# A recurrence on one core: the hidden product of half B from bf16 parts in every step, its input part placed by DMA, its gate product in fp32

## The chip, the core and the metric

The kernel runs on one core of one Trainium2 chip. Its time is the device time in microseconds, and the kernel before takes 1639.37 us, the median of three runs (1638.94 to 1640.77). The engines are TensorE (PE, with its weight loads as PEld), VectorE (DVE), ScalarE (ACT), GpSimd (POOL) and SyncE (SP), which only issues DMAs here.

## The reference

```
def step(h, x_t):                        # 512 steps, batch 8, 512 units
    fused = sigmoid(concat([x_t, h]) @ w_W + w_b)
    r, z = split(fused, 2)
    m = x_t @ wx_W + wx_b + r * (h @ wh_W + wh_b)
    return z * h + (1 - z) * tanh(m)
out = x + (h after every step)
```

Everything is fp32. Each step needs the state of the step before, so the 512 steps come one after the other; in each, the state (8 x 512) is multiplied with three 512 x 512 matrices (hh with wh_W, z and r with the lower half of w_W). The products of x need no state.

## The kernel before, in words

**Layout.** The 512 units are four chunks of 128 (k = 0 to 3 as inputs, j = 0 to 3 as outputs). Half A of the outputs is chunks 0 and 1 of the next state, half B chunks 2 and 3. The state is the stationary operand: 32 columns, which hold 4 steps x 8 batches, with zeros but for one step's eight. Output quarter j goes to rows 32j to 32j + 31 of a PSUM bank, so four quarters of the array work side by side, and a VectorE transpose of 128x64 in blocks of 32 turns the result back into the layout of the state. Four steps are a group g; a bank holds the x part of a group for all its four steps.

**Banks.** Per group and parity: A (192 columns: hh, z, r of half A), B (128 columns: r and hh of half B) and C (64 columns in the bank `cs`: z of half B). In odd groups C is fp32 like A and B. In even groups from step 24 on (`in_parts`, L500), C is made from bf16 parts (`parts`, L442): GpSimd splits the state into three bf16 parts, eight columns each (24 in all), TensorE multiplies these with the three parts of the weights (`wb`, `w2`, `w3`; one weight load, then three matmuls, two of them by `kept` without a load), and VectorE sums the parts after the transpose with a `tensor_reduce` (L692). Each step of such a group has its own cell in `cs`, filled beforehand with its x part times a mask (`spread_c`, L503).

**One step of TensorE** (L626 to 647): the products in the order `A0 B0 A1 A2 A3 B1 B2 B3 C0 C1 C2 C3` (bank, chunk of the state), then a share of the x products for later groups (`x_step`, L585). The share is by u, the step's number within eight: 384 columns for u = 0 to 3, 288 for u = 4 to 7 (`SHARE`). u = 0 to 3 are the even group of the eight steps, u = 4 to 7 the odd one.

**The recurrence** (L667 to 758): of each half, `turn_r`, `turn_h`, `turn_z` transpose on VectorE, and the two gates get their sigmoid on ScalarE. `memory` is a scan on VectorE over two slots for each unit: slot 0 starts from hh, slot 1 multiplies with r and adds the x part (`md0` holds 0 and r, `md1` holds hh and x), then a tanh on ScalarE. `update` is a scan that makes the new state in `hT`. `update(0, 0)` makes chunk 0, which A0 and B0 of the next step need; `update(0, 1)` chunk 1; `update(1, 0)` and `update(1, 1)` chunks 2 and 3. All of VectorE's, ScalarE's and SP's instructions run in program order.

**Between.** `spread` copies a group's x part into the banks (ScalarE), `turn_x` transposes the x part of m into `md1` (VectorE). Sums of x products go through `even` and `odd` in SBUF; the last addition for rows 64 to 127 of `even` is made by VectorE at u = 5, those for rows 0 to 63 by ScalarE at u = 2. The last two groups read PSUM directly (`source`). `Flow` (L92) plans the semaphores: for PSUM an instruction waits for the last access of every other engine to the same bank and rows; DMAs go round 24 lanes. All instructions of the loop are recorded under L255, so the tiles' names tell them apart: `tr`, `tz` are turned gates, `tzB` and `tzs` the turned and summed parts of C, `hd0` the sigmoid of z, `m` the scan's result.

Of the kernel before, what the change touches and what calls it, by code (L numbers as in the profile page):

```python
# [8 lines left out]
F32 = mybir.dt.float32  # L9
# [14 lines left out]
DVE_FILL = 14  # L24
IDLE = 3
ORDER = "A0 B0 A1 A2 A3 B1 B2 B3 C0 C1 C2 C3"

FIRST = "A0 A1 A2 A3 x x x x B0 B1 B2 B3 C0 C1 C2 C3"

BANKS = {"A": 192, "B": 128, "C": 64}  # L30
# [19 lines left out]
XP = {"A": slice(0, 192), "X": slice(192, 320), "C": slice(320, 384), "B": slice(384, 512)}  # L50
# [214 lines left out]
def tile_cond_rnn_residual(  # L265
# [105 lines left out]
    def wh(bank, k, j):  # L371
        return wa[:, k, j] if bank == "A" else wb[:, k, j, {"C": slice(0, 64), "B": slice(64, 192)}[bank]]
# [11 lines left out]
    split = [const.tile([P, NQ, 3, B], F32, name=f"split{i}") for i in range(2)]  # L384
    w2 = const.tile([P, NQ, NQ, HU], F32, name="w2")
    w3 = const.tile([P, NQ, NQ, HU], F32, name="w3")
    mask = const.tile([P, GS, 32], F32, name="mask")

    md0 = [[pair(n, f"md0{n}{i}", 32, 2) for i in range(2)] for n in "AB"]
    md1 = [[pair(n, f"md1{n}{i}", 32, 2) for i in range(2)] for n in "AB"]  # L390
# [12 lines left out]
    for n, t_ in enumerate(hd0[0] + hd0[1] + md0[0] + md0[1] + hs):  # L403
        (nc.vector if n < DVE_FILL else nc.gpsimd).memset(t_, 0.0)
    steps = const.tile([P, GS, 32], F32, name="steps")
    nc.vector.memset(steps, 0.0)
    for n in range(GS):
        nc.vector.memset(steps[:, n, B * n : B * n + B], 1.0)
    nc.vector.transpose(mask.rearrange("p s n -> p (s n)"), steps.rearrange("p s n -> p (s n)"))
# [12 lines left out]
    def state(hf, i, slot=2):  # L422
# [8 lines left out]
         "B": wide[q]["B"][:, : BANKS["B"]],  # L431
         "C": cs[:, GS * HU : GS * HU + HU]}
# [9 lines left out]
    def parts(out_, i, k, j):  # L442
        lhsT = high(split[i % 2])[:, k].rearrange("p u b -> p (u b)")[:, 1::2]
        for n, t_ in enumerate((wb[:, k, j, :HU], w2[:, k, j], w3[:, k, j])):
            (nc.tensor.kept if n else mm)(out_, lhsT, high(t_)[:, 1::2])
# [15 lines left out]
    bias = const.tile([P, 512], F32, name="bias")  # L461
    for hf in range(2):
# [40 lines left out]
    def spread_c(g, steps_):  # L503

        for s in steps_:
            nc.scalar.activation(
                cell(GS * g + s), source(g)[:, XP["C"]], AF.Copy, scale=mask[:, s, :1]
            )

    def turn_x(g, hf):  # L510

        c0 = XP["X"].start + HU * hf
        nc.vector.transpose(
            md1[hf][g % 2][:, :, :, 1].rearrange("p n c -> p c n"), source(g)[:, c0 : c0 + HU]
# [89 lines left out]
    for k in range(NQ):  # L604
        for g in range(3):
            take(first[g], 1)
        if k == 0:
            mm(wide[1]["B"], ones.rearrange("p j m -> p (j m)"), rows4, start=True)
            nc.vector.tensor_copy(bias, wide[1]["B"])
            for t_ in (even, odd):  # L610
# [3 lines left out]
    spread_c(0, range(GS))  # L614
    for hf in range(2):
        turn_x(0, hf)
    keep(1)
    keep(2)
# [4 lines left out]
    for i in range(T):  # L623
# [8 lines left out]
        for n in (ORDER if i else FIRST).split():  # L632
# [4 lines left out]
            lhsT = hs[i % NH][:, k, :32, 2]  # L637
            for j in range(NQ):
                if bank == "C" and in_parts(i):
                    parts(cell(i)[32 * j : 32 * j + 24], i, k, j)  # L640
                else:
                    to = cell(i) if bank == "C" else ps[bank]
                    mm(to[32 * j : 32 * j + 32, :], lhsT, wh(bank, k, j))
# [7 lines left out]
        def scan(c_, out_, d0, d1):  # L651
# [10 lines left out]
            "h": (pa[:, :HU], ps["B"][:, HU:]),  # L662
            "z": (pa[:, HU : 2 * HU], cell(i)),
# [281 lines left out]
```

## Time and profile before

| | |
|---|---|
| median of three runs | 1639.37 us |
| the profiled execution, whole | 1637.59 us |
| its span, first to last instruction | 1635.5 us |
| granted TensorE clock | 1.00 |
| TensorE busy | 1625.4 us |
| VectorE, ScalarE, GpSimd busy | 1235.8, 1254.0, 531.8 us |
| DMA: out, by 128 issues | 64 KB each, 1.6 us to landing |
| DMA: x, by 112 issues | 64 KB each, 2.4 us to landing |

A timeline row gives the start in us, the time from the first start to the last end of the instructions merged into it, the engine, the line, the operation, the tiles (out<-in), the shape and the count; a bracket at its end tells how long the engine stood idle before it and for whom. A row of groups gives, after the count, the busy time of all in us and the mean of one in ns, then the idle time before them.

### The profile page before, as it was taken

Reading aid. Unit: us, or ns where it says so; the run is one execution under the profiler, and the core shown is the slowest. Engines: PE = TensorE matmul, PEld = TensorE weight load, DVE = VectorE, ACT = ScalarE, POOL = GpSimd, SP = SyncE. Lnnn points to the kernel's source line nnn. Section 1 sums busy time; section 2 is a strip of 40 time slices with the busy share of each in tenths; the row PEclk is TensorE's granted clock in tenths of the full one; section 3 lists DMA queues with packets and bytes.
Section 4 is the critical chain, followed back from the end, with each engine's and each line's share of the span. In section 5 each row is a group of like instructions: output and inputs, shape, how many; then the busy total and the mean of one; then the engine's idle time right before and its main releaser. Section 6 shows DMA issues by size and latency. Waiting matters only on the chain.

```text
span 1635.5 us, 127307 instructions
## 1 busy us (share of the span) xinstructions
PE 1625.4 (99%) x58202; PEld 1397.4 (85%) x50394; DVE 1235.8 (76%) x9433; ACT 1254.0 (77%) x6188; POOL 531.8 (33%) x2272
## 2 busy tenths in 40 slices
PE   8999999999999999999999999999999999999998
PEld 5988898988888888888888888888888888988887
DVE  7777777777777777777777777777777777777776
ACT  4777777778777777777777777777777777777775
POOL 1323323333233333332333333323333333333332
PEclk9999999999999999999999999999999999999999
DMA  4000000000000000000000000000000000000000
GB/s 185 12 14 18 15 15 14 18 15 14 15 18 15 15 14 18 15 15 15 17 15 15 15 18 14 15 15 18 14 15 15 17 15 15 15 18 10 10 10 11
DMA packets 37297, 31.25 MB, mean 19 GB/s; under 512 B 4084, under 2 KB 35060, under 8 KB 36600
## 3 DMA queue, kind: packets, MB, share of 16 engines
q1 hardware_dynamic: 36576, 22.89, 4.5%
q8 instruction: 425, 6.96, 1.7%
q14 instruction: 144, 1.18, 0.2%
q10 hardware_dynamic: 152, 0.22, 0.0%
HBM read 14.70 MB, written 8.39 MB: 14 GB/s over the span
## 4 chain that ended last, share of the span: by engine, by line
PE 98%; DVE 1%; DMA 0%; ACT 0%; issue 0%; DVEq 0%; ACTq 0%; SPq 0%
PE A L255 41%; PE B L255 27%; PE xp L255 17%; PE cs L255 9%; PE cs L219 4%; PE eps L255 1%; DMA head<-in_xh_dram 0%; DVE tr L255 0%; DVE m L255 0%; DVE tw L255 0%; DVE hT L255 0%; DVE md1A L255 0%; DVE tz L255 0%; DVE md1B L255 0%; DVE even L255 0%
## 5 line engine op out<-in xcount | busy, mean ns | idle before, releaser
L255 PE MATMUL A<-wa,hT 128*32 128x192 f32 x16384 | 872.3, 327 | 3.2 <-DVE hT L255 3.1
L255 PEld LDWEIGHTS A<-wa,hT 128*32 128x32 f32 x16384 | 549.4, 122 | 189.8 <-DVE hT L255 132.1
L255 PE MATMUL B<-wb,hT 128*32 128x128 f32 x16384 | 652.0, 273 | 0.0
L255 PEld LDWEIGHTS B<-wb,hT 128*32 128x32 f32 x16384 | 542.5, 122 | 19.9 <-DMA wb<-in_wb_dram 0.3
L255 POOL TENSOR_TENSOR ot<-xin,hT 128x16 f32<-128x16 f32 x991 | 224.1, 250 | 598.8 <-DVE hT L255 596.8
L255 ACT ACTIVATE hT<-m 128x8 f32<-128x8 f32 x2048 | 349.2, 208 | 65.0 <-DVE m L255 64.1
L255 DVE STREAM_TRANSPOSE tr<-A 128x64 f32<-128x64 f32 x512 | 127.9, 250 | 291.9 <-PE A L255 285.8
L255 PE MATMUL xp<-tw,sx 128*32 128x384 f32 (+2 forms) x1464 | 264.0, 433 | 0.0
L255 POOL TENSOR_TENSOR split<-hT 128x32 f32<-128x32 f32 x488 | 126.0, 258 | 410.0 <-DVE m L255 397.9
L255 ACT ACTIVATE hT<-hT 128x16 f32<-128x16 f32 x1022 | 210.3, 225 | 50.1 <-DVE hT L255 47.8
L255 ACT ACTIVATE md0A<-tr 128x16 f32<-128x16 f32 x512 | 112.2, 219 | 165.4 <-DVE tr L255 158.8
L255 DVE TENSOR_TENSOR_SCAN hT<-hd0B,hT 128x24 f32<-128x24 f32 x1024 | 179.5, 204 | 75.7 <-ACT hT L255 52.4
L255 PE MATMUL xp<-wx,xin 128*32 128x384 f32 (+4 forms) x1348 | 218.3, 413 | 0.0
L255 DVE TENSOR_TENSOR_SCAN hT<-hd0A,hT 128x24 f32<-128x24 f32 x1024 | 198.3, 194 | 0.0
L255 PE MATMUL cs<-wb,hT 128*32 128x64 f32 x8576 | 173.0, 219 | 0.0
L255 PEld LDWEIGHTS cs<-wb,hT 128*32 128x32 f32 x8576 | 161.4, 122 | 0.0
L255 DVE TENSOR_TENSOR_SCAN m<-md0A,md1A 128x16 f32<-128x16 f32 x1024 | 142.3, 181 | 6.9
L255 DVE TENSOR_TENSOR_SCAN m<-md0B,md1B 128x16 f32<-128x16 f32 x1024 | 145.0, 163 | 0.6 <-issue 0.4
L255 ACT ACTIVATE hd0A<-tz 128x16 f32<-128x16 f32 x512 | 116.0, 227 | 20.9
L219 PE MATMUL cs<-w,split 128*24 128x64 bf16 x7808 | 129.9, 192 | 0.0
L255 PE MATMUL cs<-wb,split 128*24 128x64 bf16 x3904 | 122.2, 192 | 0.0
L255 POOL TENSOR_TENSOR split<-split 128x16 f32<-128x16 f32 x488 | 105.2, 216 | 38.2
(101 smaller groups left out, 2216.0 us busy)
## 6 DMA issues: line engine op xcount, KB each, us to landing
out_dram<-ot SPq DMA_DIRECT2D x128, 64.0 KB, 1.6
xin<-in_x_dram SPq DMA_DIRECT2D x112, 64.0 KB, 2.4
wx<-in_wx_dram SPq DMA_DIRECT2D x4, 768.0 KB, 7.5
wa<-in_wa_dram SPq DMA_DIRECT2D x4, 384.0 KB, 10.1
wb<-in_wb_dram SPq DMA_DIRECT2D x1, 1152.0 KB, 13.4
xin<-in_x_dram SPq DMA_DIRECT2D x3, 256.0 KB, 3.1
wb<-in_wb_dram SPq DMA_DIRECT2D x1, 384.0 KB, 13.8
head<-in_xh_dram ACTq DMA_DIRECT2D x1, 208.0 KB, 5.6
```

The source lines that it names most:

```text
L219: return t.add_instruction(mybir.InstMatmult(name=self.nc.get_next_instruction_name(), ins=[t.lower_ap(rhs), t.lower_ap(lhsT)], outs=[t.lo ...
L255: inst = getattr(self, item.op, getattr(engine, item.op, None))(*item.args, **item.kw)
```

## The change

- Bank B now holds z and r of half B, in fp32. The third product is H: hh of half B, into cells of `cs` (eight now, one for each step of eight). It is fp32 until step 23 and from parts in all steps from 24 on.
- The split state has four columns for each batch, (batch, part), the fourth zero: 32 columns instead of 24. GpSimd makes it in every step (before step 24 it copies the state into the second column).
- After the transpose a unit has four neighbouring slots. `memory` of half B is a scan over these four with factors 0, 1, 1 and r: it sums the three parts, multiplies with r and adds what stands in the fourth, which is the x part. The `tensor_reduce` goes, and so does the transpose of x of half B.
- The x part must stand in every fourth row of the cell. `move_x` sends 16 DMAs a group (4 steps x 4 quarters, 8 rows x 64 elements each) from `even` or `odd` to a tile `xz`, whose other rows hold the bias of hh in the first row of four and zeros. `fill(i + 2)` copies one 128x64 piece of `xz` to the cell on ScalarE, in every step, behind the last update; it takes the place of `spread_c` and of the copies of C.
- In each step `turn_z(1)` now stands before `update(0, 0)` and `turn_h(1)` behind it, the order of updates is the same in all steps. The third bias addition (`keep(2)`) moves from the start into step 1.

```diff
-ORDER = "A0 B0 A1 A2 A3 B1 B2 B3 C0 C1 C2 C3"
+ORDER = "A0 B0 A1 A2 A3 B1 B2 B3 H0 H1 H2 H3"
-BANKS = {"A": 192, "B": 128, "C": 64}
+BANKS = {"A": 192, "B": 128}
...
+    def products_h(i, k):
+        four = split[i % 2]
+        for j in range(NQ):
+            to = cell(i)[32 * j : 32 * j + 32]
+            if not in_parts(i):
+                mm(to, four[:, k].rearrange("p b u -> p (b u)"), wh("H", k, j))
+                continue
+            lhsT = high(four)[:, k].rearrange("p b u -> p (b u)")[:, 1::2]
+            for n, t_ in enumerate((wh("H", k, j), w2[:, k, j], w3[:, k, j])):
+                (nc.tensor.kept if n else mm)(to, lhsT, high(t_)[:, 1::2])
...
     def cell(i):
-        return cs[:, HU * (i % GS) : HU * (i % GS) + HU] if i // GS % 2 == 0 else banks[1]["C"]
+        return cs[:, HU * (i % NH) : HU * (i % NH) + HU]
     def in_parts(i):
-        return 3 * NH <= i < T and i // GS % 2 == 0
+        return 3 * NH <= i < T
+    def move_x(g):
+        at = (even, odd)[g % 2]
+        if source(g) is not at:
+            nc.scalar.copy(at[:, XP["M"]], source(g)[:, XP["M"]])
+        for s in range(GS):
+            for j in range(NQ):
+                r = 32 * j
+                (nc.sync if g or s else nc.scalar).dma_start(
+                    out=xz[g % 2][r + 3 : r + 32 : 4, s],
+                    in_=at[r + B * s : r + B * s + B, XP["M"]],
+                )
+    def fill(i):
+        if i < T:
+            nc.scalar.copy(cell(i), xz[i // GS % 2][:, i % GS])
...
         def memory(hf, q):
             c_ = slice(q, q + 1)
-            scan(c_, ms[hf], md0[hf][g % 2][:, rows], md1[hf][g % 2][:, rows])
-            act(state(hf, i, 1)[:, :, c_], ms[hf][:, :, c_, 1], AF.Tanh)
+            d1 = memB.rearrange("p c (n s) -> p n c s", s=4) if hf else md1[g % 2][:, rows]
+            scan(c_, ms[hf], md0[hf][g % 2][:, rows], d1)
+            act(state(hf, i, 1)[:, :, c_], ms[hf][:, :, c_, SL[hf] - 1], AF.Tanh)
...
         turn_r(1)
+        turn_z(1)
+        update(0, 0)
         turn_h(1)
-        update(0, 0)
...
+        nc.after(update(0, 1), r_done[1])
...
+        memory(1, 0)
+        memory(1, 1)
         update(1, 0)
         update(1, 1)
-        if 0 < o < LAST and u == 1:
-            spread(2 * o + 1, "C")
-        if nxt and u in (6, 7):
-            spread_c(2 * o + 2, (2 * u - 12, 2 * u - 11))
+        for n in (1, 2) if i == 0 else () if i == T - 6 else (i + 1, i + 2) if i == T - 5 else (i + 2,):
+            fill(n)
...
         if o == LAST:
             if u == 2:
+                move_x(2 * o + 1)
...
         elif u == 5:
             if sums:
                 nc.vector.tensor_tensor(even[HI, XC], reg(BE), both[HI], ALU.add)
+            if sums or o + 1 == LAST:
+                move_x(2 * o + 2)
...
         elif u == 7 and nxt:
             if o:
                 nc.scalar.copy(odd[LO, XC], reg(GA))
-            turn_x(2 * o + 2, 1)
+            if sums:
+                move_x(2 * o + 3)
```

More of the change, by code (lines that the diff above doesn't have):

```diff
@@ L402, in tile_cond_rnn_residual @@
     nc.scalar.activation(const.tile([P, 1], F32, name="table"), zeros[:, :1], AF.Sigmoid)
-    for n, t_ in enumerate(hd0[0] + hd0[1] + md0[0] + md0[1] + hs):
+    for n, t_ in enumerate(hd0[0] + hd0[1] + md0[0] + md0[1] + split + hs):
         (nc.vector if n < DVE_FILL else nc.gpsimd).memset(t_, 0.0)
[L405 to L409, printed above, removed]
+    for t_ in md0[1]:
+        nc.gpsimd.memset(t_[:, :, :, 1:3], 1.0)
+    fourth = const.tile([P, 32], F32, name="fourth")
+    nc.vector.memset(fourth, 0.0)
+    nc.vector.memset(fourth[:, ::4], 1.0)
+    nc.vector.transpose(mask, fourth)
     for t_ in hd0[0] + hd0[1]:
@@ L670, in turned @@
             return t_[:, :, rows], inst
+        memB = work.tile([P, 2, 32], F32, tag="memB", name=f"memB_{i}")
         r_done = [None, None]
```

156 lines of the change are left out of this document (71 added, 85 removed).

## The prediction

> **What bounds the kernel now.** I read the page first: the span, the busy shares and the chain that ended last.
>
> ```profile
> span 1635.5 us, 127307 instructions
> PE 1625.4 (99%) x58202; PEld 1397.4 (85%) x50394; DVE 1235.8 (76%) x9433; ACT 1254.0 (77%) x6188; POOL 531.8 (33%) x2272
> PE 98%; DVE 1%; DMA 0%; ACT 0%; issue 0%; DVEq 0%; ACTq 0%; SPq 0%
> ```
>
> TensorE is never idle and is 98% of the chain, so on this page the kernel is TensorE's stream, and any matmul time saved should come off the end. The next question is how far the recurrence, which runs beside that stream on VectorE and ScalarE, is from being the limit itself. So I read the timeline of TensorE over an fp32 step (u = 4 of the eight) and over a step that takes C from bf16 parts (u = 1):
>
> ```profile
> 714.91 0.62 PE L255 MATMUL cs<-wb,hT 128*32 128x64 f32 x31
> 715.36 0.41 PE L255 MATMUL xp<-tw,xin 128*32 128x288 f32 x2
> 715.85 0.55 PE L255 MATMUL A<-wa,hT 128*32 128x192 f32 x8
> 716.17 0.44 PE L255 MATMUL B<-wb,hT 128*32 128x128 f32 x8
> 716.39 1.20 PE L255 MATMUL A<-wa,hT 128*32 128x192 f32 x24
> 718.02 0.62 PE L255 MATMUL cs<-wb,hT 128*32 128x64 f32 x31
> ...
> 730.64 0.20 PE L255 MATMUL cs<-wb,split 128*24 128x64 bf16 x2
> 731.00 0.49 PE L255 MATMUL xp<-wx,xin 128*32 128x384 f32 x2
> 731.65 0.54 PE L255 MATMUL A<-wa,hT 128*32 128x192 f32 x8
> ```
>
> Starts matter here, since matmuls overlap. C in fp32 holds TensorE from 714.91 to 715.36, 0.45 us; from parts it holds it from 730.64 to 731.00, 0.36 us. The x work behind it takes 0.49 us (288 columns) in the one and 0.65 us (384 columns) in the other. A0 to the end of B is 718.02 - 715.85 = 2.17 us in both. So an fp32 step is 2.17 + 0.45 + 0.49 = 3.11 us, a parts step 2.17 + 0.36 + 0.65 = 3.18 us. The same from VectorE, by the first transpose of u = 0, of u = 4 and of the next u = 0:
>
> ```profile
> 727.07 0.25 DVE L255 STREAM_TRANSPOSE tr<-A 128x64 f32<-128x64 f32 x1 [0.80 <-PE A L255]
> ...
> 739.79 0.25 DVE L255 STREAM_TRANSPOSE tr<-A 128x64 f32<-128x64 f32 x1
> ...
> 752.22 0.25 DVE L255 STREAM_TRANSPOSE tr<-A 128x64 f32<-128x64 f32 x1 [0.81 <-PE A L255]
> ```
>
> The four parts steps take 12.72 us, 3.180 each, and the four fp32 steps 12.43 us, 3.108 each.
>
> Now the loop beside it: the end of A, VectorE's transposes and scans, the first new state, A0 of the next step, the end of A again. The last steps of the kernel have no x work left to fill TensorE, so there the loop alone sets the pace:
>
> ```profile
> 1622.06 0.55 PE L255 MATMUL A<-wa,hT 128*32 128x192 f32 x8 [0.24 <-DVE hT L255]
> 1625.14 0.55 PE L255 MATMUL A<-wa,hT 128*32 128x192 f32 x8 [0.24 <-DVE hT L255]
> ```
>
> These are fp32 steps, TensorE waits 0.24 us in each, and and A0 comes 3.08 us after A0. That is the row of the whole argument: taking matmuls away cannot bring an fp32 step below 3.08 us, and it stands at 3.108 already. Only 0.03 us of each is TensorE's to give.
>
> **Part by part. The product of half B.** From step 24 on, 244 steps had C from parts and 244 in fp32; now all 488 take it from parts. By the rows above, 0.45 - 0.36 = 0.09 us less of TensorE in each of the 244 that change (u = 4 to 7), 22 us if nothing else held them. z of half B now rides in bank B, which stays 128 columns wide: nothing there. The stationary part grows from 24 to 32 columns:
>
> ```profile
> L255 PEld LDWEIGHTS cs<-wb,split 128*24 128x24 bf16 x3904 | 107.4, 93 | 9.9
> ```
>
> A load stands before three matmuls on the same quarter of the array and runs under its neighbours. At worst the first of a step shows its longer length, 93 x 32/24 - 93 = 31 ns, in the 244 steps that TensorE still bounds: 0 to 7.6 us. I take 0, since the row's loads are covered; more columns cannot gain. [...]
>
> **The loop.** VectorE in the same fp32 step, and TensorE's weight load that follows:
>
> ```profile
> 715.25 0.23 DVE L255 STREAM_TRANSPOSE tr<-B 128x64 f32<-128x64 f32 x1
> 715.40 0.24 DVE L255 STREAM_TRANSPOSE md1B<-B 128x64 f32<-128x64 f32 x1
> 715.53 0.20 DVE L255 TENSOR_TENSOR_SCAN hT<-hd0A,hT 128x24 f32<-128x24 f32 x1
> 715.65 0.23 DVE L255 STREAM_TRANSPOSE tz<-cs 128x64 f32<-128x64 f32 x1
> 715.79 0.17 DVE L255 TENSOR_TENSOR_SCAN hT<-hd0A,hT 128x24 f32<-128x24 f32 x1
> ...
> 716.33 0.31 DVE L255 TENSOR_TENSOR_SCAN hT<-hd0B,hT 128x24 f32<-128x24 f32 x2 [0.20 <-ACT hT L255]
> ```
>
> ```profile
> 715.78 0.24 PEld L255 LDWEIGHTS A<-wa,hT 128*32 128x32 f32 x8 [0.25 <-DVE hT L255]
> ```
>
> The first update (715.53 to 715.73) lets A0's weights load, at 715.78, and A0 starts at 715.85. With C shortened TensorE would be ready for A0 at 715.85 - 0.09 = 715.76: it would stand waiting. In front of that update the change puts the transpose of z (from B, to a plain tile) where hh's stood (from B, into every second slot). After the plain ones the next instruction starts 0.15 us later (715.25 to 715.40, 715.65 to 715.79 is 0.14), after the slotted one 0.13 (715.40 to 715.53). So the update moves 0.02 us back, and the floor from 3.08 to 3.10 us. The four u = 4 to 7 steps then take 4 x 3.10 = 12.40 instead of 12.43 us: 61 x 0.03 = 1.8 us gained. Bounds: no delay at all, 3.08, 61 x 0.11 = 6.7 us gained; the 0.05 us more that a plain transpose could cost, 3.13, 61 x 0.09 = 5.5 us lost.
>
> **Behind the first update** lie the four-slot scans. Sixteen elements take 163 ns, 24 take 194:
>
> ```profile
> L255 DVE TENSOR_TENSOR_SCAN m<-md0B,md1B 128x16 f32<-128x16 f32 x1024 | 145.0, 163 | 0.6 <-issue 0.4 <-DVE tzB L255 0.2
> L255 DVE TENSOR_TENSOR_SCAN hT<-hd0A,hT 128x24 f32<-128x24 f32 x1024 | 198.3, 194 | 0.0
> ```
>
> Thirty-two are then 0.02 to 0.06 us longer than 16. They delay A2. In the fp32 step above both updates of half B are done at 716.64, and A2 starts one chunk of A after A1, at 716.39 + 0.32 = 716.71: the second of them has 0.07 us to spare and A2 needs only the first. Against A0, which now comes 0.02 us later in the loop, A2 keeps its place, so this is covered. If it were not, 0.04 us would come on 244 steps, 10 us. In the u = 0 to 3 steps the sum over the quarter (reduce) and a mixed order go away; A2 is sometimes late there, and 3.180 goes to 2.17 + 0.36 + 0.65 = 3.176 at best: 244 x 0.004 = 1.0 us gained.
>
> **ScalarE and the DMAs.** One 128x64 fill a step, against five pieces in eight steps before; TensorE's parts on POOL in every step, not every second, behind the update and done before H0 of the next step, with 67% of POOL free. The new wait is on ScalarE: fill(i+2) waits for four DMAs, and the state copies, the spreads and the next sigmoid are queued behind it; VectorE and then TensorE wait for that. It is tight at one place, u = 6 of each eight, whose x is finished by VectorE only in u = 5:
>
> ```profile
> 719.78 0.56 DVE L255 TENSOR_TENSOR even<-xp,both 64x384 f32<-64x384 f32 x1
> ```
>
> ```profile
> 714.25 0.33 SPq L255 DMA_DIRECT2D out_dram<-ot  x1
> 714.62 0.43 SPq L255 DMA_DIRECT2D xin<-in_x_dram  x1
> ```
>
> ```profile
> out_dram<-ot SPq DMA_DIRECT2D x128, 64.0 KB, 1.6
> xin<-in_x_dram SPq DMA_DIRECT2D x112, 64.0 KB, 2.4
> ```
>
> ```profile
> 722.65 0.55 ACT L255 ACTIVATE cs<-even,mask 128x64 f32<-128x64 f32 x2
> 723.63 0.26 ACT L255 COPY B<-even 128x128 f32<-128x128 f32 x1
> 724.25 0.22 ACT L255 ACTIVATE md0A<-tr 128x16 f32<-128x16 f32 x1 [0.35 <-DVE tr L255]
> ```
>
> Two of the four DMAs read rows 0 to 63, ready since u = 2, and SP, which runs ahead, has sent them. The other two go at 720.4 and, an issue being 0.37 us, 720.8; with 1.6 to 2.4 us to landing, the last is there at 722.4 to 723.2. The fill is due at 722.65, so it waits 0 to 0.6 us. Behind it ScalarE needs 723.89 - 722.65, less 0.25 us for the one of the two old fills that is gone, 1.0 us, before 724.25: it can bear a wait to 723.25. So I take 0. [...] No run here has yet shown such an eight-row DMA.
>
> **Ends.** At the start the third bias addition and one transpose leave VectorE ahead of the first step, against a longer queue on SP:
>
> ```profile
> 16.76 0.56 DVE L255 TENSOR_TENSOR even<-eps,bias 128x384 f32<-128x384 f32 x1 [0.76 <-ACT cs L255]
> ```
>
> That is 0 to 0.8 us gained, with the wait; I take 0.4. In the last group two fills come at once, one step after their x is copied: eight issues, 7 x 0.37 + 1.6 to 7 x 0.43 + 2.4, is 4.2 to 5.4 us where 3.1 and 0.1 to 0.6 us of ScalarE's idle time are there: 0.5 to 2.2 us lost, I take 1.1.
>
> **Sum.** -1.8 - 1.0 - 0.4 + 1.1 = -2.1 us. The profiled execution took 1637.59 us, 2.1 us around its span, and lies 1.78 us below the median of 1639.37. On its own time that is 1635.5; on the median 1637.3, rounded to **1637.0**. What this kernel's measurement can tell from no change is about 0.2%, 3.3 us: the forecast is within it.
>
> **Rivals.** (1) *The loop is shorter than I think*: the transpose swap costs nothing and the floor stays 3.08. Then -6.7 - 1.0 + 0.7, 1632. For it: the 0.02 us is at the edge of what the rows resolve. Chance 0.24; a floor that falls further, to TensorE's 3.02 us, gives 1639.4 - 22 - 0.3 = 1617, and the tail's 3.08 speaks against it: 0.05. (2) *Slower, by the fill of u = 6*: the wait for DMAs takes the place of the multiplied copies. It decides when the last row lands after 723.25, 2.45 us after its issue, or when SP is not ahead and all four go after 720.4 (0.75 us more: 723.1 to 723.9). Each 0.1 us beyond costs 61 x 0.1 = 6 us; a middle of 0.3 gives 18 us, 1655, the end 0.65 us, 40 us. For it: the landing of 2.4 us in the row. Against: that one reads from DRAM. Chance 0.13. (3) *Slower, by a longer loop* (floor 3.13, or scans on A2): 5 to 10 us, 1642 to 1648. Against: every plain transpose from B or cs shows 0.15. Chance 0.13.
>
> **Numbers.** My case, 1634 to 1641, has 0.45. Faster by over 0.2% (below 1636.1): 0.29 of rival 1 and a quarter of my case, 0.40. Within 0.2%: the rest of my case, 0.34, and a few of rival 3, 0.37. Slower: 0.23. The range leaves out TensorE's 3.02 and the long end of rival 2, and something for what I don't see: 1629 to 1651.
>
> **What would show it.** Right: VectorE's transposes of A 3.10 us apart in u = 4 to 7 and 3.18 in u = 0 to 3; weight loads of A waiting for hT in u = 4 to 7, and A0 behind them, with H0 to x 0.36 us. Wrong: steps of 3.02 there; ScalarE waiting for DMAs in u = 6 with a late sigmoid in u = 7; A2 rather than A0 late; H longer than 0.36 us.

## The result and the profile after

The changed kernel takes 1926.05 us (median of six, 1919.19 to 1934.57), the kernel before on the same chip 1639.03 (six, 1638.00 to 1640.77): a ratio of 1.1753, 95% interval 1.1714 to 1.1793. The forecast was 1637.0, the top of its range 1651. The profiled execution took 1920.54 us. Its page, with the span, the busy times, the chain that ended last (by engine, then by line) and the costliest group whose idle time is new:

```profile
span 1918.7 us, 131377 instructions
PE 1730.9 (90%) x62106; PEld 1347.9 (70%) x46490; DVE 1226.9 (64%) x9063; ACT 1234.3 (64%) x6382; POOL 780.1 (41%) x3296
...
PE 37%; SPq 32%; DVE 12%; DMA 9%; ACT 5%; issue 4%; DVEq 0%; ACTq 0%; POOL 0%
SPq L255 32%; PE A L255 20%; PE B L255 9%; DMA xz<-odd 6%; PE xp L255 4%; DMA xz<-even 3%; DVE m L255 2%; DVE tr L255 2%; ACT hT L255 2%; PE cs L219 2%; DVE odd L255 2%; DVE tz L255 2%; DVE hT L255 1%; ACT xp L255 1%; PE cs L255 1%
...
L255 DVE TENSOR_TENSOR odd<-xp,both 64x384 f32<-64x384 f32 x61 | 33.6, 551 | 204.2 <-DMA xz<-odd 204.2
```

TensorE's share of the chain fell from 98% to 37%, and 32% is now SPq: SP issuing DMAs. The last row says where the two meet. VectorE's addition into `odd`, once in eight steps (u = 3), stands 204.2 us for the DMAs that copy `odd` to `xz`. The waits view names who stands behind it:

```profile
DVE odd L255 <- DMA xz<-odd: 204.2, 61, 5.1
...
PEld xp L255 <- DVE odd L255: 138.4, 61, 4.0
PE xp L255 <- DVE odd L255: 127.3, 61, 3.8
...
ACT cs L255 <- DMA xz<-even: 42.4, 68, 2.1
```

(us in total, times, longest.) All 61 additions wait, and TensorE's x products of u = 4 wait for them. The wait is a write after a read: `odd` may not be overwritten before the 16 DMAs of `move_x`, issued from u = 7 of the eight steps before, have read it. Why they are so late is in SP's timeline (start, us, DMAs merged into the row):

```profile
839.93 16.70 SPq L255 DMA_DIRECT2D xz<-even  x15
856.67 10.66 SPq L255 DMA_DIRECT2D xz<-odd  x16
867.43 0.39 SPq L255 DMA_DIRECT2D out_dram<-ot  x1
867.86 1.02 SPq L255 DMA_DIRECT2D xin<-in_x_dram  x1
868.92 0.43 SPq L255 DMA_DIRECT2D out_dram<-ot  x1
869.39 0.43 SPq L255 DMA_DIRECT2D xin<-in_x_dram  x1
869.87 15.71 SPq L255 DMA_DIRECT2D xz<-even  x16
```

Sixteen DMAs take 10.66 us. From start to start that is 0.667 each, of which 0.625 is the issue itself; the issue of a store or a load of 128 rows takes 0.43 in the median. SP is issuing for 77% of the time between steps 24 and 504. The row of 15.71 us has one wait in it: behind its first two issues SP stands until the addition into `even` has ended (875.2). On VectorE at the same time:

```profile
864.96 0.37 DVE L255 TENSOR_TENSOR_SCAN hT<-hd0B,hT 128x24 f32<-128x24 f32 x2 [0.17 <-ACT hT L255]
868.60 0.55 DVE L255 TENSOR_TENSOR odd<-xp,both 64x384 f32<-64x384 f32 x1 [3.27 <-DMA xz<-odd]
869.20 0.24 DVE L255 STREAM_TRANSPOSE tr<-A 128x64 f32<-128x64 f32 x1
```

The last DMA out of `odd` has been issued at 856.67 + 10.66 = 867.33; the addition starts 1.27 us later. Everything of the next step is queued behind it, beginning with the transpose of A.

These rows close a loop that is longer than TensorE's eight steps. The addition into `even` ends in u = 5, at 875.2; the 14 DMAs of `even` still to issue end at 869.87 + 15.71 = 885.58 (10.4 us); the 16 of `odd` take 10.7; the landing 1.3; the addition into `odd` 0.55; two steps to the next addition into `even` about 6. Together 29 us, where eight steps of TensorE's work take 25.2. SP's issues alone would fit into these: 32 at 0.667 and four loads and stores are some 23 us. What does not fit is SP's wait for the addition into `even`, 5.7 us in the median, in front of the sixteen DMAs of `odd`. Eight steps measure 29.6 in the table. It gives the mean step by its place u in the eight, in ns, from VectorE's first transpose of A, steps 24 to 503:

| u | 0 | 1 | 2 | 3 | 4 | 5 | 6 | 7 | eight |
|---|---|---|---|---|---|---|---|---|---|
| before | 3185 | 3186 | 3185 | 3190 | 3104 | 3109 | 3115 | 3117 | 25191 |
| after | 3233 | 3290 | 3223 | 6145 | 3806 | 3333 | 3200 | 3378 | 29608 |

Sixty eights at 4.417 us more are 265 us of the 283.2 by which the span grew: u = 3 gives 177, u = 4 and 5 give 56, u = 6 and 7 give 21, u = 0 to 2 give 11. The start to step 24 gives 14, the end 4.

u = 4 and 5 are paid to TensorE's clock. In 36 of the sixty eights a stretch at half clock lies in u = 4, which then takes 4.22 us in the median; in the other 24 it takes 3.16. By stretch of time, at the end of one stall (columns: busy us and instructions of TensorE, its weight loads, VectorE, ScalarE and GpSimd, then the granted clock, the DMAs' share and GB/s):

```profile
1605.30:1608.30 3.00, 0.88 (x68) 0.65 (x28) 0.55 (x1) 0.00 (x0) 0.37 (x2) 1.00 0.11 30
1608.30:1609.30 1.00, 0.83 (x8) 0.16 (x8) 0.94 (x10) 0.63 (x4) 0.00 (x0) 0.74 0.52 148
1609.30:1610.30 1.00, 0.69 (x12) 0.44 (x16) 0.83 (x7) 0.70 (x7) 0.34 (x2) 0.50 0.12 32
1610.30:1611.30 1.00, 1.00 (x20) 0.72 (x16) 0.32 (x4) 0.90 (x5) 0.69 (x4) 0.50 0.08 18
1611.30:1612.60 1.30, 1.30 (x28) 0.91 (x24) 0.00 (x0) 0.00 (x0) 0.61 (x3) 0.66 0.00 0
```

TensorE is idle for most of the first row, and the clock falls to 0.50 when its work is back. The trace has 39 such stretches of 3.413 us, all starting on one grid of 3.413 us. Between steps 20 and 500, every grid interval with 1.87 us or more of TensorE idle time (37 of 520) is followed by one at 0.50, and none with 1.78 or less is. In the run with 16-row DMAs further down the line is less sharp: every interval followed by 0.50 has 1.98 us or more, but one with 2.28 is not followed by it. In the changed kernel, then, a little over half an interval of idle time was enough.

What the prediction asked to look at: the loop in u = 4 to 7. Two transposes of A with the first update between them, H on TensorE, and the weight loads of the step between:

```profile
872.36 0.25 DVE L255 STREAM_TRANSPOSE tr<-A 128x64 f32<-128x64 f32 x1 [0.88 <-PE A L255]
...
873.37 0.20 DVE L255 TENSOR_TENSOR_SCAN hT<-hd0A,hT 128x24 f32<-128x24 f32 x1
...
875.52 0.25 DVE L255 STREAM_TRANSPOSE tr<-A 128x64 f32<-128x64 f32 x1 [0.17 <-PE A L255]
```

```profile
875.93 0.21 PE L255 MATMUL cs<-wb,split 128*32 128x64 bf16 x4
...
876.28 0.33 PE L255 MATMUL xp<-tw,xin 128*32 128x192 f32 x2
```

```profile
873.63 0.19 PEld L255 LDWEIGHTS A<-wa,hT 128*32 128x32 f32 x8 [0.20 <-DVE hT L255]
...
874.58 0.51 PEld L255 LDWEIGHTS A<-wa,hT 128*32 128x32 f32 x16 [0.22 <-DVE hT L255]
```

H takes 0.35 us, as forecast. The step takes 3.16, not 3.10: the second weight row (A2 and A3) waits 0.22 us for half B's state, which the step of before did not do. Two groups tell why:

```profile
L255 DVE TENSOR_TENSOR_SCAN hT<-hd0B,hT 128x24 f32<-128x24 f32 x1024 | 185.3, 220 | 86.8 <-ACT hT L255 86.8
...
L255 DVE TENSOR_TENSOR_SCAN m<-md0B,memB 128x32 f32<-128x32 f32 x1024 | 173.9, 212 | 0.0
```

The four-slot scan takes 212 ns where the two-slot one took 163, and half B's update 220 where it took 204. Half B has two updates, and A2 needs the first. In u = 4 to 7 that one has a median of 269 ns, against 208 in the kernel before, and an operation of GpSimd lies beside it, the second part of its split of half A:

```profile
874.25 0.23 POOL L255 TENSOR_TENSOR split<-split 128x16 f32<-128x16 f32 x1
```

```profile
874.26 0.37 DVE L255 TENSOR_TENSOR_SCAN hT<-hd0B,hT 128x24 f32<-128x24 f32 x2 [0.17 <-ACT hT L255]
```

### The profile page after: what moved, and what is told of

It is laid out like the page before. It is cut to its first block, busy times and chain, and to the rows that moved or that the text cites. A ratio compares the mean times of both kernels' runs of the same rounds, so it can differ in the third digit from the quotient of the medians.

```text
span 1918.7 us, 131377 instructions
## 1 busy us (share of the span) xinstructions
PE 1730.9 (90%) x62106; PEld 1347.9 (70%) x46490; DVE 1226.9 (64%) x9063; ACT 1234.3 (64%) x6382; POOL 780.1 (41%) x3296
## 3 DMA queue, kind: packets, MB, share of 16 engines
q14 instruction: 174, 1.43, 0.3%
## 4 chain that ended last, share of the span: by engine, by line
PE 37%; SPq 32%; DVE 12%; DMA 9%; ACT 5%; issue 4%; DVEq 0%; ACTq 0%; POOL 0%
SPq L255 32%; PE A L255 20%; PE B L255 9%; DMA xz<-odd 6%; PE xp L255 4%; DMA xz<-even 3%; DVE m L255 2%; DVE tr L255 2%; ACT hT L255 2%; PE cs L219 2%; DVE odd L255 2%; DVE tz L255 2%; DVE hT L255 1%; ACT xp L255 1%; PE cs L255 1%
## 5 line engine op out<-in xcount | busy, mean ns | idle before, releaser
L255 PE MATMUL A<-wa,hT 128*32 128x192 f32 x16384 | 933.8, 343 | 45.4 <-DVE hT L255 44.7
L255 PEld LDWEIGHTS A<-wa,hT 128*32 128x32 f32 x16384 | 524.7, 126 | 327.5 <-DVE hT L255 264.7
L255 POOL TENSOR_TENSOR split<-hT 128x32 f32<-128x32 f32 x976 | 256.3, 263 | 985.2 <-DVE hT L255 976.3
L255 PE MATMUL cs<-wb,split 128*32 128x64 bf16 (+1 forms) x8576 | 258.2, 196 | 7.4 <-ACT cs L255 6.0
L219 PE MATMUL cs<-w,split 128*32 128x64 bf16 x15616 | 257.5, 193 | 0.1
L255 POOL TENSOR_TENSOR split<-split 128x16 f32<-128x16 f32 x976 | 225.2, 231 | 76.4
L255 PEld LDWEIGHTS cs<-wb,split 128*32 128x32 bf16 (+1 forms) x8576 | 222.8, 98 | 35.8 <-ACT cs L255 9.4
L255 PE MATMUL xp<-tw,xin 128*32 128x288 f32 x976 | 114.5, 334 | 127.3 <-DVE odd L255 127.3
L255 DVE TENSOR_TENSOR_SCAN m<-md0B,memB 128x32 f32<-128x32 f32 x1024 | 173.9, 212 | 0.0
L255 DVE TENSOR_TENSOR odd<-xp,both 64x384 f32<-64x384 f32 x61 | 33.6, 551 | 204.2 <-DMA xz<-odd 204.2
L255 DVE TENSOR_TENSOR_SCAN m<-md0A,md1A 128x16 f32<-128x16 f32 x1024 | 142.2, 181 | 29.9 <-ACT md0A L255 23.7
```

The lines of the kernel that those rows point to most:

```text
L219: return t.add_instruction(mybir.InstMatmult(name=self.nc.get_next_instruction_name(), ins=[t.lower_ap(rhs), t.lower_ap(lhsT)], outs=[t.lo ...
L255: inst = getattr(self, item.op, getattr(engine, item.op, None))(*item.args, **item.kw)
```

## The experiments

The runs were on several chips; each time is compared with the kernel before, run beside it on the same chip (1640.88 to 1648.31 us).

### Who waits: ScalarE at u = 6, or VectorE at u = 3

The theory W: the addition into `odd` waits for its readers, SP's queue being too long. The rival F: what hurts is ScalarE waiting in its fills.

**Late fill.** Each PSUM copy one step later. In this kernel and the next, step 3 takes the x part of group 2, since its copy now stands behind the DMAs that overwrite it.

```diff
-        for n in (1, 2) if i == 0 else () if i == T - 6 else (i + 1, i + 2) if i == T - 5 else (i + 2,):
+        for n in (i + 1,):
             fill(n)
```

> The changed kernel with each fill emitted one step later (fill(i + 1) behind step i). Theory W (VectorE's addition into odd at u = 3 waits until all sixteen DMAs have read odd, and SP issues these eight-row DMAs only every 0.667 us): the wait at u = 3 stays, some 3 us in each eight steps, and only ScalarE's waits for xz go; 1900 to 1920 us. Rival F (my second rival: it is the fill of u = 6 that costs): the time falls under 1700 us.

Measured: 1954.52 us in a single run.

```profile
DVE odd L255 <- DMA xz<-odd: 224.7, 60, 5.0
ACT cs L255 <- DMA xz<-even: 22.0, 2, 20.4
```

ScalarE's 68 waits shrank to 2, and VectorE's wait stayed. F falls. u = 6 and 7 are back at a mean of 3182 and 3189 ns, and u = 3 and 4 take 6618 and 4116 instead: what ScalarE no longer waits for, the longer loop through SP takes back. The time is 34 us above W's bracket. Against the trace of the changed kernel the steps from 24 on are 25 us longer, the start 12 us, with a single stall of 20.4 us at step 3, and the end 4 us shorter.

**Staging tile and late fill.** GpSimd copies the 64 columns to a tile of their own, and the DMAs read that: `odd` is free as soon as the copy is done. The 32 DMAs stay as they are.

```diff
-        at = (even, odd)[g % 2]
-        if source(g) is not at:
-            nc.scalar.copy(at[:, XP["M"]], source(g)[:, XP["M"]])
+        at = stage[g % 2]
+        nc.gpsimd.tensor_copy(at, source(g)[:, XP["M"]])
...
-                    in_=at[r + B * s : r + B * s + B, XP["M"]],
+                    in_=at[r + B * s : r + B * s + B],
```

> As e1_late, and GpSimd first copies the 64 columns to a tile of their own, from which the DMAs read; odd and even are free again after that copy. Theory W: the wait at u = 3 goes, TensorE keeps its full clock, and what stays is the slower loop of u = 4 to 7 (3.16 us a step instead of 3.11): 1640 to 1665 us. Rival L (the mass of small DMAs loads SP or the engines' memory, whoever waits): stays over 1850 us.

Measured: 1709.42 us, ratio 1.0371 (1.0329 to 1.0413). The wait of VectorE for a DMA is gone from the waits, the granted clock is back at 0.994, and u = 3 is at a median of 3186 ns. With the late fills, ending that wait takes the ratio from 1.1753 to 1.0371. The time is 44 us above the bracket; a one-off 19.4 us is the start-up stall again, and the rest is the subject of the last group of experiments.

**No DMAs.** This kernel leaves out the x part of half B's memory: `xz` stays as it was filled at the start.

```diff
-                (nc.sync if g or s else nc.scalar).dma_start(
-                    out=xz[g % 2][r + 3 : r + 32 : 4, s],
-                    in_=at[r + B * s : r + B * s + B, XP["M"]],
-                )
+                pass
```

> The changed kernel without the DMAs of move_x, so the x part of the memory of half B is left out. It prices all of the change but the DMAs. Theory W: the steps of u = 4 to 7 at 3.16 us, those of u = 0 to 3 at 3.18: 1639 + 61 x 4 x 0.05 - 1 = 1650 us, 1645 to 1655. If the bf16 products or the four-slot scan cost more than that by themselves: over 1680 us. If my forecast of the rest was right: 1637.

Measured: 1662.36 us, ratio 1.0086 (1.0060 to 1.0112). That is 14 us over the kernel before on its chip (1647.94), where 6 to 16 were expected over 1639; u = 4 to 7 have medians of 3167 to 3183 ns, u = 0 to 3 of 3178 to 3187 (before 3180 to 3184). The DMAs and those who wait for them are nearly the whole loss.

### Why an issue takes 0.667 us

**16-row DMAs.** The same 32 DMAs with twice the rows and the same queueing; the x parts land in other rows than the ones they belong to.

```diff
-                    out=xz[g % 2][r + 3 : r + 32 : 4, s],
-                    in_=at[r + B * s : r + B * s + B, XP["M"]],
+                    out=xz[g % 2][r + 1 : r + 32 : 2, s],
+                    in_=at[r + 16 * (s // 2) : r + 16 * (s // 2) + 16, XP["M"]],
```

> The changed kernel with as many DMAs, each with 16 rows instead of 8 (x lands in other rows than it should). Theory R (an issue costs 0.667 us because there are only eight rows): 0.37 to 0.47 us an issue as with 128 rows, the sixteen of odd are through before u = 3 needs it, 1645 to 1670 us. Rival S (it is SBUF to SBUF in 256-byte rows that costs): 0.667 us stays, and 1900 us or more.

Measured: 2099.18 us in a single run, granted clock 0.928; an issue every 0.633 us in the median, but one in twenty takes over 1.43 us, and the waits are longer:

```profile
DVE odd L255 <- DMA xz<-odd: 288.6, 62, 5.7
ACT cs L255 <- DMA xz<-even: 133.9, 131, 2.7
```

Theory R expected 0.37 to 0.47 us. With twice the rows an issue costs about the same, so few rows are not what makes it dear.

**Before with DMAs.** The kernel before, with 32 DMAs of eight rows in each eight steps to a tile that nobody reads; `dmas(0)` stands in u = 5, `dmas(1)` in u = 7.

```diff
+    def dmas(q):
+        for s in range(GS):
+            for j in range(NQ):
+                r = 32 * j
+                nc.sync.dma_start(
+                    out=sink[r + 3 : r + 32 : 4, GS * q + s],
+                    in_=zeros[r + B * s : r + B * s + B, :HU],
+                )
```

> The kernel before, with the change's 32 eight-row DMAs in each eight steps added (from a tile of zeros to a tile that nobody reads), issued at u = 5 and u = 7; no engine waits for them. Theory W (it is the waiting that costs): the time of before, within 0.5%, with an issue every 0.667 us. Rival L (so many small DMAs slow the other engines or the fetching of instructions): over 3% slower.

Measured: 1657.68 us, ratio 1.0107 (1.0087 to 1.0128): between the 0.5% of W and the 3% of L. The median steps are those of before to 8 ns, in every u. The load of the DMAs costs 1.1% here; being waited for costs most of the rest.

**Six forms.** The kernel before, with three DMAs of each of six forms in each eight steps: `pp` from 8 rows to 8 rows of SBUF, `qq` from 8 to every fourth of 32, `rr` from 32 to every fourth of 128, `ss` 128 rows, all SBUF to SBUF; `tt` 8 rows and `uu` 128 rows from DRAM.

```diff
+                    (t_[0:8, m], zeros[0:8, :HU]),
+                    (t_[3:32:4, m], zeros[0:8, :HU]),
+                    (t_[3:128:4, m], zeros[0:32, :HU]),
+                    (t_[:, m], zeros[:, :HU]),
+                    (t_[0:8, m], x[8][0:8, :HU]),
+                    (t_[:, m], x[8][:, :HU]),
```

> The kernel before, with six forms of DMA added at u = 5, three of each in a row, waited for by nobody: SBUF to SBUF 8 rows to 8 neighbouring rows (pp), 8 rows to every fourth row (qq), 32 rows to every fourth row (rr), 128 rows (ss); DRAM to SBUF 8 rows (tt), 128 rows (uu); all in 256-byte rows. It measures the issue alone. Sixteen rows were not cheaper than eight (0.63 us), so theory S (SBUF to SBUF costs the sequencer 0.6 us, DRAM to SBUF 0.4): pp, qq, rr, ss at 0.6 or more, tt and uu at 0.35 to 0.45. Rival D (few rows are dear whatever the source): tt like qq at 0.62, ss like uu at 0.4.

```profile
805.71 2.50 SPq L255 DMA_DIRECT2D frr<-zeros  x3
808.30 3.55 SPq L255 DMA_DIRECT2D fss<-zeros  x3
811.95 1.94 SPq L255 DMA_DIRECT2D ftt<-in_x_dram  x3
...
822.79 2.30 SPq L255 DMA_DIRECT2D fpp<-zeros  x3
825.14 1.96 SPq L255 DMA_DIRECT2D fqq<-zeros  x3
```

Each row is three issues with the pauses between them. The medians of a single issue are 0.693 (`pp`), 0.624 (`qq`), 0.511 (`rr`), 0.594 us (`ss`), against 0.296 (`tt`) and 0.354 (`uu`). The run took 1650.68 us (a single run). D falls: the issue is 2.1 to 2.3 times as dear from SBUF to SBUF as from DRAM with 8 rows, and 1.7 times with 128. S has the order right, but `rr` and `ss` are under its 0.6 and `tt` under its 0.35. The 0.37 us of the prediction came from rows with DRAM on one side. The source is not the whole of it, though: in the next kernel a DMA from DRAM that fills 32 rows of `xz` has a median of 0.666 us, and one of 64 rows to DRAM 0.501. What in a form sets its price was not separated further.

### Other ways to bring x over, and the loop

**Through DRAM.** For each group two DMAs write 64 rows to DRAM and four read them back into every fourth row: 12 DMAs in eight steps in place of 32. The PSUM copies are one step later, with the order at the start kept (so also in the kernels below that have DMAs, except the one with early fills).

```diff
+                w = nc.sync.dma_start(out=scr[g % 4, half], in_=at[half, XP["M"]])
...
+                    rd = nc.sync.dma_start(
+                        out=xz[g % 2][32 * j + 3 : 32 * j + 32 : 4],
+                        in_=scr[g % 4, 32 * j : 32 * j + 32].rearrange("(s b) c -> b s c", s=GS),
+                    )
```

> The changed kernel with x moved by six DMAs a group instead of sixteen (each half of odd or even written to DRAM by one DMA of 64 rows, then read back by one DMA for each quarter, all four steps at once), and each fill one step later. Theory W: SP needs some 8 us in each eight steps, no wait at u = 3, full clock: like the kernel without the DMAs, 0.9% over before, between 0.5% and 2%. Rival L: over 3%.

Measured: 1670.28 us, ratio 1.0180 (1.0165 to 1.0195). It lies in W's bracket. With 12 DMAs SP has time, issuing for 39% of it, and VectorE waits for none; u = 4 to 7 stand at medians of 3165 to 3181. ScalarE now and then waits for the rows that come back:

```profile
ACT cs L255 <- DMA xz<-scr_dram: 16.2, 14, 2.4
```

For these waits above all u = 0 has a mean of 3353 ns with a median of 3180, 10 us in all over the 60 eights. It is the same in the next kernel (3345, 3184).

**Through DRAM, one split.** As the last, but GpSimd splits both halves of h at once behind the last update, in two operations instead of four, so that none of them lies beside half B's scans.

```diff
-            ks, s1 = slice(2 * hf, 2 * hf + 2), B * ((i + 1) % GS)
+            ks, s1 = slice(0, NQ), B * ((i + 1) % GS)
...
```

> As e6_bounce, and GpSimd splits both halves of the state at once, behind the last update, so that its second operation no longer runs beside the update of chunk 2 (262 ns beside it, 208 without). Theory P (this overlap lengthens the loop of u = 4 to 7): those steps 0.05 us shorter, 61 x 4 x 0.05 = 13 us less than e6_bounce, about the time of before. Rival: the split then comes too late for H0, steps longer than in e6_bounce.

Measured: 1660.87 us, ratio 1.0116 (1.0099 to 1.0133). That is 9.4 us less than the last, where 13 were expected. u = 4 to 7 have medians of 3104, 3106, 3122 and 3104, within 12 ns of those of before. Half B's updates are at their old length, the first of them at a median of 208 ns again:

```profile
L255 DVE TENSOR_TENSOR_SCAN hT<-hd0B,hT 128x24 f32<-128x24 f32 x1024 | 166.0, 204 | 86.7 <-ACT hT L255 86.7
```

The four-slot scans are as long as in the changed kernel (224 and 199 ns in u = 4 to 7, before 166 and 169). So the longer loop was the meeting of GpSimd's split with half B's update, 61 ns, and without it the four-slot scan is covered.

**Staging tile, one split**, late fills, and **staging tile, one split, early fills** (the fills where the change has them), to price the wait of ScalarE alone. The edits are those of the staging tile and of one split; the second keeps the change's line of fills.

> The whole change, all 32 eight-row DMAs per eight steps included, with three things moved: GpSimd copies the 64 columns into a tile of their own and the DMAs read that, each PSUM copy is done one step later, and GpSimd splits both halves at once. Theory W (the lost time is the addition that waits for its operand's readers, the loss at u = 6 and the loop): no wait of VectorE for a DMA in the waits, and what is left is the load of the DMAs themselves, 1.1% where they were added to the kernel before and nobody waited for them: 1.008 to 1.02, or 1654 to 1673 us on a chip where before takes 1640. Rival F (the issues and packets themselves hold the kernel up, in whatever order): 1.04 or more.

> As the kernel with the staging tile and the merged split, but with the PSUM copies where the change has them, two steps ahead, so that the copy in u = 6 needs the DMAs that are issued after u = 5. It prices that wait alone. Theory W: ScalarE waits there in nearly every eight steps for about 1 to 1.6 us, and u = 7 or the next step is longer by 0.5 to 1.5 us, 30 to 90 us in all over the kernel with the later copies: 1.03 to 1.07 of before. Rival C (that copy is covered, as was forecast): within 0.4% of the kernel with the later copies.

Measured on one chip: 1695.24 us, 1.0281 (1.0267 to 1.0296), and 1764.04, 1.0704 (1.0667 to 1.0742). Of the second:

```profile
ACT cs L255 <- DMA xz<-stage: 167.0, 119, 3.4
```

In it u = 7 is at a median of 4361 ns, 1.26 us above before; with late fills ScalarE waits 6.3 us in all. VectorE waits for a DMA in neither. The early fill costs 69 us here, so C falls for this kernel. It is not what the early fill costs in the changed kernel. Here all four DMAs of that fill stand behind GpSimd's copy and go 0.34, 1.04, 1.71 and 2.38 us after the addition into `even`, and the fill of u = 6 waits 1.84 us in the median. In the changed kernel two of the four have gone before that addition, the last goes 0.70 us after it, and the fill waits 0.17 us in the median. The first of the two kernels lies above its bracket of 1.008 to 1.02, and what is over is not in these waits but in gaps of TensorE, by the table below.

### What is left

**No DMAs, one split**, the two edits together, run on two chips. It has, to 12 ns, the kernel before's median step in every u (3180 to 3182, 3105, 3105, 3122, 3105).

> The kernel after without the eight-row DMAs (it leaves out the x part of half B's memory), and with GpSimd splitting both halves of h at once behind the last update instead of one half beside each. Theory P (without the DMAs only the loop of steps u = 4 to 7 is longer, by the GpSimd operations that lie beside half B's scans; the rest of the change nets to nothing): the kernel with only the DMAs left out stood at 1.0086 of the kernel before, and 0.06 us x 4 x 60 = 14 us or 0.9% go, so 0.997 to 1.003, with medians of 3.10 to 3.12 us for u = 4 to 7 and 3.18 for u = 0 to 3. Rival Q (the four-slot scans and the other moved work cost something in every step besides): 1.005 or more, with u = 4 to 7 still above 3.14.

Measured: 1663.27 us, ratio 1.0089 (1.0074 to 1.0103). Neither P nor Q: the medians are P's, the time is Q's. The excess lies in single steps, 37 of them more than 0.3 us above their median. TensorE in one of these gaps, on the second chip:

```profile
1113.06 0.21 PE L255 MATMUL cs<-wb,split 128*32 128x64 bf16 x4
1113.09 0.24 PE L219 MATMUL cs<-w,split 128*32 128x64 bf16 x6
1113.90 0.19 PE L219 MATMUL cs<-w,split 128*32 128x64 bf16 x1 [0.57 <-issue]
```

TensorE stops in the middle of H, between two matmuls that wait for nothing. Count every record of TensorE, its matmuls, weight loads and semaphore instructions, and take a gap from one start to the next. Then all the gaps over 350 ns of steps 24 to 503 in this kernel on the first chip stand at the same place, record 193 of a block of 256 (so also the 13 of the kernel with no DMAs, the 17 of before with DMAs and 68 of the 69 of the staging tile with one split). The DMA view has a queue of kind "instruction" with 426 packets of 16 KB, one for each 256 records of TensorE, and nearly every gap there ends 1.2 to 1.6 us after such a packet has landed. The fixed place and the packets speak for TensorE standing there for want of instructions; no row shows the fetch itself. Three runs on one chip, among them the kernel before itself and this kernel with H from fp32 in half of the steps:

```diff
-        return 3 * NH <= i < T
+        return 3 * NH <= i < T and i // GS % 2 == 0
```

> The kernel before, for its trace on the chip of the two runs beside it. In the kernel with the change but without its DMAs and with the merged split, the time over the kernel before lies in single gaps of TensorE, each at record 193 of a block of 256 TensorE records, 1.2 to 1.6 us after a 16 KB instruction packet has landed. Theory S (TensorE stands for want of instructions there, and the change makes that more frequent): here under 10 us of such gaps over 150 ns, and the packet starts 0.3 us or more sooner after the preceding block's first record than in the changed kernel. Rival C (it is the chip, not the change): 15 us or more of such gaps here too.

> The same kernel as e8_no_dma_split (it leaves out the x part of half B's memory), beside the kernel before on one chip: 1.007 to 1.011 again. Theory S: its own gaps over 150 ns at record 193 of the block, less those of the kernel before on this chip, are the difference of the two times to 5 us. Rival C: the gaps of the two are alike and the difference lies elsewhere.

> The same kernel with the 16 products of column H from fp32 in the steps u = 4 to 7, as the kernel before has them, and from parts only in u = 0 to 3 (it leaves out the x part of half B's memory, and in u = 4 to 7 the fp32 product takes in what the parts left in the other rows). The number of TensorE's instructions is the same, 64 per step for column H, in about 0.45 us where the parts take 0.36. Theory D (the parts drain a block of instructions faster, and so the next block comes late): less than half of e8's gaps, and 0.998 to 1.004 of the kernel before. Rival O (the parts have nothing to do with it; the packets start later for another cause, such as the order of the work or fewer waits of the sequencer): gaps within a quarter of e8's, 1.006 or more.

| kernel | us over before, same chip | gaps over 150 ns at that record | us in them |
|---|---|---|---|
| before, chip of the result | | 3 | 0.8 |
| before, chip of these three | (a single run, 1645.31) | 23 | 6.5 |
| no DMAs, one split, there | 8.5 | 45 | 16.8 |
| the same with H in fp32 at u = 4 to 7, there | 7.6 | 33 | 11.1 |
| no DMAs, one split, first chip | 15.0 | 62 | 22.8 |
| no DMAs | 14.4 | 36 | 11.9 |
| before with DMAs | 16.8 | 42 | 13.7 |
| six forms | 9.8 | 33 | 10.6 |
| through DRAM | 29.4 | 26 | 8.5 |
| through DRAM, one split | 20.0 | 51 | 17.5 |
| staging tile, late fill | 61.5 | 72 | 29.9 |
| staging tile, one split | 46.9 | 110 | 48.2 |

In the kernels whose loop is longer (no DMAs, through DRAM, staging tile with late fill) or whose ScalarE waits (both through DRAM), the gaps are only a part of what is over. Measured on the three: 1645.31 us (a single run), 1656.17 (ratio 1.0043, 1.0027 to 1.0060) and 1655.26 (1.0044, 1.0030 to 1.0059). The second was expected at 1.007 to 1.011 again and lies below: the same kernel stands at 1.0089 on one chip and 1.0043 on another. Their profiled executions took 1645.31, 1655.3 and 1650.66: differences of 10.0 and 5.3 us, where the gaps differ by 10.2 and 4.6. So S holds for the place of the time: what was left of the change without its DMAs is TensorE standing at record 193 of its blocks, some of it the chip's and some the change's. The waits view shows the same on the chip of these three, first of the kernel before, then of the kernel with no DMAs and one split:

```profile
PEld xp L255 <- issue: 5.8, 24, 0.8
PEld cs L255 <- issue: 3.1, 10, 0.5
```

```profile
PEld xp L255 <- issue: 14.2, 39, 1.5
PEld cs L255 <- issue: 9.2, 23, 0.8
```

Why the change makes these gaps more frequent isn't settled. The packet starts later: counting blocks from record 193, a median of 0.62 and 0.81 us after the first record of the preceding block in the kernel before on the two chips, 0.91 in the one beside it (1.03 on the first chip), 1.01 in before with DMAs, 1.21 in the staging tile with one split. Between the first two of one chip (0.81 and 0.91) that is far less than the 0.3 us S expected. Whether small DMAs delay it these rows don't show, since the kernel without DMAs stands at 1.03 on the first chip. Nor do they settle the density of the parts: with H back in fp32 at u = 4 to 7 the gaps are a quarter fewer, not the half that theory D wanted, and the median time is the same, between the two brackets; but of the gaps that the kernel before doesn't have, 22 went to 10, in an execution that was the fastest of its eight.

## Why the prediction was wrong

- **"an issue being 0.37 us"** is the step that failed. An issue of these DMAs takes 0.667 us. At 32 in eight steps that is 21.3 of 25.2 us, with four loads and stores between them. The nearest rows were of another kind, 64 KB between DRAM and SBUF, and the doubling of their price was nowhere in the bounds. What it decides can be estimated from the rows: in the kernel before 18.6 us pass from the addition into `even` to the next into `odd`. Behind the first stand 30 issues and 1.3 us to landing. At 0.37 us they are through after 12.4 us and the addition into `odd` does not wait; at 0.667 they need 21.3.
- **Who waits for a moved read.** The price did its harm at a place that the prediction did not have. The part on ScalarE and the DMAs ("tight at one place, u = 6 of each eight") looked for those who wait for `xz` and left out those who want to write `even` and `odd`: this wait stood at nothing, without a reason. A copy on ScalarE had read these tiles in some half a microsecond (two multiplied copies take 0.55 us, 722.65 in the kernel before); 16 DMAs hold `odd` for the 10.66 us of their issues and 1.27 us more, until the last has landed. This wait, with the clock behind it, made the 233 us of u = 3 to 5.
- **Rival 2** had the right event, at about its price, and it was the smaller part. That SP "runs ahead" held at its place: in all 59 eights SP had sent two of the four DMAs before the addition into `even` and stood waiting for it, and the next went 0.03 us after it. The fill of u = 6 waits 0.17 us in the median and up to 2.1 in single eights; u = 6 and 7 together lost 21 us, where the rival had 18 for its middle and 40 for its end. With all four behind the addition, its other condition, the fill costs 69 us in the kernel with the staging tile.
- **The loop.** The swap of transposes cost nothing, where 0.02 us was taken: the first update starts 1.01 us after the transpose of A in both kernels (873.37 - 872.36 after). "A2 keeps its place" failed: u = 4 to 7 went to 3.16 us, 0.05 to 0.06 on 240 steps, 12 to 14 us where 10 was the price if it were not covered. The scan was sized well (0.05 in a range of 0.02 to 0.06) and would have been covered; what was not priced is GpSimd's split beside half B's first update, 269 for 208 ns. "Behind the update" was true of it and no excuse, because it lay beside the next one.
- **u = 0 to 3** were to gain 0.004 us a step, 1.0 us in all. The terms given, 2.17 + 0.36 + 0.65, make 3.18 and not 3.176, and in the kernels without DMAs these steps are at 3.18 as before.
- **Right:** H at 0.35 to 0.36 us for 48 parts matmuls, 7.3 to 7.5 ns each; the wider weight load at nothing (97 ns in the mean against 93, and H no longer for it); u = 0 to 3 at 3.18 when nothing stalls; and how little the steps had to give, since no median step of any kernel here came below 3.10.
- **The ends** gave 14 and 4 us, not -0.4 and 1.1. Step 0 comes 0.8 us sooner, as the bounds had it; but from step 0 to step 24 the changed kernel takes 14.4 us more than before and the kernel with no DMAs only 1.7, so most of the 14 is DMAs again.
- **Not foreseen at all:** the gaps of TensorE at one record of its instruction blocks, 10 us between two kernels whose median steps agree. Even with the stall, the early fill and the split mended, no version here beats the kernel before; the best that does all the work is at 1.0116. Not tried was issuing part of the DMAs from another engine's queue.

## What to carry to other kernels

When a copy by an engine becomes a set of DMAs, ask three questions: how many issues a period its queue can bear at the measured price of that kind of DMA (the 0.37 us of a load's issue did not hold for these DMAs from SBUF to SBUF, which took 0.667); what the queue itself waits for between them; and who next writes what they read. Here a staging tile settled the last, and fewer DMAs the first. And when medians of all steps agree and the time doesn't, look for the rare steps: they have a place and a cause of their own.

## What the runs showed of the hardware

- In the run with six forms SP took 0.51 to 0.69 us (medians) to issue a DMA from SBUF to SBUF and 0.30 to 0.35 for one from DRAM, with 8 rows and with 128. In the kernels through DRAM a DMA from DRAM into 32 rows of the staging order of `xz` took 0.67, so the source alone does not set it. Of the changed kernel's loop of 29 us the issues were 21 (32 at 0.667) and the landing 1.3.
- In the changed kernel every interval of 3.413 us with 1.87 us or more without work on TensorE (37 of 520) was followed by one at a granted clock of 0.50, and none with 1.78 or less was; in the run with 16-row DMAs one interval with 2.28 was not either.
- In the kernel before, TensorE's instructions came in 425 packets of 16 KB, one for every 256 of its records, 3.78 us apart in the median. In the kernel with no DMAs and one split TensorE stood at record 193 of a block 62 times for over 150 ns on the first chip (22.8 us in all), in the staging tile with one split 110 times (48.2 us). A single gap was up to 0.8 us, in the staging tile with one split up to 1.2, and those over 350 ns ended, nearly all, 1.2 to 1.6 us after a packet had landed.
- VectorE's first update of half B in u = 4 to 7 took a median of 269 ns in the changed kernel, with an operation of GpSimd beside it, and 208 without in the kernel through DRAM with one split (all of half B's updates: 220 and 204 on average).
